# Two small products of a two-layer convolution kernel, with the weight matrix and the data exchanged on the tensor engine

## The chip, the cores and the metric

The kernel runs on one core of a Trainium2 chip. A core has a tensor engine (PE, which loads weights into its array, PEld, and streams a moving operand past them), a vector engine (DVE), a scalar engine (ACT), GpSimd (POOL) and a queue engine (SP) that here only issues DMAs. Matmul results land in PSUM, 8 banks of 128 partitions by 512 float32; everything else works in SBUF, 128 partitions wide. The metric is the device time of one execution in microseconds, the median of several runs. Everything is float32.

## What is computed

Two layers, on x of shape (4, 256, 256, 64): 4 images, height and width 256, 64 channels.

```python
# layer 0
h  = _pw(_ln(x, g1, b1), w_te, b_te)              # 64 -> 128 channels
F  = jnp.fft.fft2(h.astype(jnp.complex64), axes=(1, 2))
fr = jnp.concatenate([jnp.real(F), jnp.imag(F)], axis=-1)
fc = jax.nn.gelu(_pw(fr, w_fc, b_fc), approximate=False)
re, im = (fc[..., :HID], fc[..., HID:])
sp = jnp.real(jnp.fft.ifft2(re + 1j * im, axes=(1, 2)))
x1 = x + _pw(sp, w_tp, b_tp)                      # 128 -> 64 channels
h2 = _pw(_ln(x1, g2, b2), w_fe, b_fe)             # 64 -> 128 channels
d  = lax.conv_general_dilated(h2, w_dw, ...) + b_dw   # depthwise 3x3
d  = jax.nn.gelu(d, approximate=False)
x  = x1 + _pw(d, w_fp, b_fp)                      # 128 -> 64 channels
# layer 1: along the height, per channel
trend = _moving_average(x, 25); seasonal = x - trend
out   = trend + irfft(first 128 modes of rfft(seasonal), mixed by w_real + 1j * w_imag)
```

`_pw` is a product over the channels, `_ln` a layer norm. The change touches the two products that go from 128 to 64 channels: with `w_tp` and with `w_fp`.

## The kernel before

Transforms are products with tables. Products are exchanged where that is linear: the projection `w_tp` is applied before the inverse transform, and `b_fp` is added only at the end of layer 1. Four generators issue the work of layer 0 in pieces (each `yield` ends one):

- `forward_h` (L313 on): loads x, normalises, transforms along the height, writes `y_d` to HBM.
- `spectral` (L387 on): the transform along the width, the mix with `w_fc`, GELU, the projection, and the inverse transform along the width, into `u_d` in HBM. It works on groups of 4 rows, two *pairs* of rows a group (the first group has three, the first of them *special*: it holds rows whose spectrum is packed as two real ones). An image has 65 pairs.
- `convolution` (L588 on): the inverse transform along the height, the residual, layer norm, the depthwise convolution, GELU, the last product, and the residual, in 32 steps of 8 columns, into `x2_d` in HBM.
- `matrices`: the 64 matrices of layer 1, at the start.

Afterwards layer 1 runs as one loop over the channels (L912 on): it loads a matrix `mt` and the columns `xc` of `x2_d`, multiplies (L932), adds `b_fp` while it empties PSUM (L944 on ACT, L946 on DVE), and stores.

**Order.** PE, DVE, ACT and POOL execute exactly in the order in which the program issues (`manual_schedule`). `spaced` gives each piece of a generator an even position on a common axis, on which an image is 1.0 long, and `merge` always takes the generator that stands furthest back. The forward part of image b is spread from b - 2.05 to b - 1.1, its spectral part from b - 1.0 to b - 0.08 in 4 x 68 pieces, its convolution from b to b + 1 in 10 x 36 pieces. So the convolution of one image, the spectral part of the next and the forward part of the one after are merged.

**The spectral step.** Step i issues four pieces: `transform_w` of pair i with `fold` of pair i - 2; `back_w` of the group that pair i - 3 closes; `mix` of pair i - 1; and then, in one piece, `project` of pair i - 2, `activate` of pair i - 1 and, at a group's end, `negate` of the next group. `transform_w` (L435) multiplies a block [real, imaginary, -real] with the tables; `negate` (L422, ACT) writes the third part. `mix` (L455) makes four banks, which ACT (L467) and DVE (L472) bring to SBUF as `g`; `activate` (L478) is the GELU on ACT, `fold` (L485) an addition on DVE and a subtraction on POOL. `project` takes its two results, `dr` and `di`, 128 hidden channels by 512 positions each, as the *stationary* operand, 128 positions at a time, and streams `w_tp` (128 x 64) past them: the positions come out on the partitions, as `back_w` (L531) needs them. That is eight matmuls of 64 moving columns into one bank, which ACT copies into `zt` (L517). The special pair also adds the bias, by a matmul of `b_tp` with `at_dc`, a row with a single one.

**The convolution step.** Step q issues ten pieces: `back_h` of chunk q with the next load; `measure` (sums on DVE, the squares on ACT, L296); `conv_first` of chunk q - 3 (products L683 and L696 into four banks, emptied by ACT L715 and DVE L717, L718); `to_channels` of q - 1 (eight transposes L648 into two banks, copied by ACT L655); `norm`; `conv_rest` (L724); `finish` for the first half of chunk q - 4; `row_sums`; `conv_rest` and `edges`; and `activate` (GELU, L741) together with `finish` for the second half. `finish` also takes the data `gs` as the stationary operand, 128 positions at a time, and streams `w_fp` (128 x 64) past it: eight matmuls (L750) into one bank, in which the positions stand on the partitions. DVE adds `x1` on the way out of PSUM (L762), into a store tile that SP writes to `x2_d` (L771).

All tiles of PSUM come from one ring of eight banks (`bank`): a new tile takes the oldest bank, and the engine that fills it waits until that bank has been emptied.

Of the kernel before, what the change touches and what calls it, by code (L numbers as in the profile page):

```python
# [11 lines left out]
F32 = mybir.dt.float32  # L12
AF = mybir.ActivationFunctionType
ALU = mybir.AluOpType
# [4 lines left out]
P = 128  # L19
N = 256  # L20
C = 64
# [86 lines left out]
def conv_seq_kernel(ctx: ExitStack, tc: tile.TileContext, a: dict, tables: bass.AP, out: bass.AP):  # L108
    nc = tc.nc
# [9 lines left out]
    def bank(name):  # L119
        return psum.tile([P, 512], F32, tag="bank", name=name)  # L120
# [4 lines left out]
    def row(ap):  # L125
        return ap.rearrange("(o n) -> o n", o=1)

    def const(shape, name):
        return consts.tile(shape, F32, tag=name, name=name)
# [26 lines left out]
    w_tp = const([P, C], "w_tp")  # L156
    nw_tp = const([P, C], "nw_tp")
    b_tp = const([1, C], "b_tp")
    at_dc = const([1, P], "at_dc")
    w_fp = const([P, C], "w_fp")  # L160
    b_fp = const([P, C], "b_fp")

    wc_main = const([P, 2, 4, HID], "wc_main")
    wc_half = const([P, 4, HID], "wc_half")
# [5 lines left out]
    with tc.tile_pool(name="prep", bufs=1) as prep:  # L170
# [13 lines left out]
        nc.sync.dma_start(w_tp, a["w_tp"])  # L184
        nc.sync.dma_start(b_tp, row(a["b_tp"]))
        nc.sync.dma_start(w_fp, a["w_fp"])
        nc.sync.dma_start(b_fp, row(a["b_fp"]).to_broadcast([P, C]))

# [22 lines left out]
        nc.vector.tensor_scalar(v_dc, ps[:, 0:1], b_te, NPOS, ALU.add, ALU.mult)  # L213
        nc.vector.tensor_scalar(nw_tp, w_tp, -1.0, None, ALU.mult)
        nc.vector.tensor_scalar(b_tp, b_tp, 2.0 * NPOS, None, ALU.mult)
        nc.vector.memset(at_dc, 0.0)
        nc.vector.memset(at_dc[:, 0:1], 1.0)


        w_fe = prep.tile([P, HID], F32, tag="w_fe", name="w_fe")  # L220
# [166 lines left out]
    def spectral(b, pool):  # L387
# [1 line left out]
        y_d = y_ds.pop(b)  # L389
        u_d = spill.tile([P, N, 2, C], F32, tag="u_d", name=f"u_d_{b}")  # L390
        u_ds[b] = u_d
        KG = 4
        groups, per_group = {}, {}

        def load_group(g):
# [90 lines left out]
            pr["d"] = [gt[:, 0] for gt in pr["gts"]]  # L486

        def project(pr):
            dr, di = pr["d"]
            zt = groups[pr["g"]]  # L490
            ps = bank(f"ps_z_{pr['n']}")
            zv = ps.rearrange("p (j q c) -> p j q c", j=2, c=C)
            lhs = lambda d, j, t: d[:, j * N + t * P : j * N + (t + 1) * P]
            if pr["special"]:

                for t in range(2):
                    for r, terms in enumerate(
                        (((dr, 0, w_tp), (di, 1, nw_tp)), ((di, 0, w_tp), (dr, 1, w_tp)))
                    ):
                        dst = zv[:, 0, 2 * t + r, :]  # L500
                        bias = t == 0 and r == 0
                        for i, (d, j, w) in enumerate(terms):
                            nc.tensor.matmul(
                                dst, lhs(d, j, t), w, start=i == 0, stop=i == 1 and not bias
                            )
                        if bias:
                            nc.tensor.matmul(dst, at_dc, b_tp, start=False, stop=True)
                nb = 1
            else:
                nb = len(pr["blocks"])  # L510
                for r, d in enumerate((dr, di)):
                    for j in range(nb):
                        for t in range(2):
                            nc.tensor.matmul(  # L514
                                zv[:, j, 2 * t + r, :], lhs(d, j, t), w_tp, start=True, stop=True
                            )
            nc.scalar.copy(  # L517
                zt.rearrange("p t r k c -> p k (t r) c")[:, pr["slot"] : pr["slot"] + nb],
                zv[:, 0:nb],
            )  # L520

        def back_w(g):
# [38 lines left out]
                slot += 1 if prs[-1]["special"] else 2  # L561
        load_group(0)
        negate(0)
        for i in range(len(prs) + 3):
            if i < len(prs):
                pr = prs[i]
                pr["blocks"] = per_group[pr["g"]][pr["i"]]
                transform_w(pr)
                if pr["last"] and pr["g"] + 1 < NG:
                    load_group(pr["g"] + 1)  # L570
            if 0 <= i - 2 < len(prs):
                fold(prs[i - 2])
            yield
            if 0 <= i - 3 < len(prs) and prs[i - 3]["last"]:
                back_w(prs[i - 3]["g"])
            yield
            if 0 <= i - 1 < len(prs):
                mix(prs[i - 1])
            yield
            if 0 <= i - 2 < len(prs):  # L580
                project(prs[i - 2])
            if 0 <= i - 1 < len(prs):
                activate(prs[i - 1])
            if i < len(prs) and prs[i]["last"] and prs[i]["g"] + 1 < NG:
                negate(prs[i]["g"] + 1)
            yield

    def convolution(b, pool):  # L588
# [1 line left out]
        u_d = u_ds.pop(b)  # L590
        W = 8
        NCH = N // W
        TD, XN = 4, 1
        NP = W // 2
        x1s, ucs, var, xns, ts, stores = {}, {}, {}, {}, {}, {}
        rows = lambda t: t.rearrange("p t w c -> p (t w) c")

        def load(q):
# [31 lines left out]
        def measure(q):  # L630
            var[q] = statistics(pool, rows(x1s[q]), f"c_{b}_{q}")
# [94 lines left out]
        def edges(q):  # L726
            for par, g in enumerate(gs[q]):
                lo, hi = 0, NP
                if q == 0 and par == 0:
                    nc.vector.tensor_tensor(g[:, 0], g[:, 0], edge_cols[:, 0], ALU.add)  # L730
                    lo = 1
                if q == NCH - 1 and par == 1:
                    hi = NP - 1
                    nc.vector.tensor_tensor(g[:, hi], g[:, hi], edge_cols[:, 1], ALU.add)
                ends = g[:, lo:hi, 0 : N : N - 1]
                nc.vector.tensor_tensor(ends, ends, edge_rows[:, lo:hi], ALU.add)  # L736

        def activate(q):
            for g in gs[q]:
# [3 lines left out]
        def finish(q, i0):  # L743

            ps = bank(f"ps_f_{b}_{q}_{i0}")
            pv = ps.rearrange("p (t w c) -> p t w c", t=2, c=C)
            for t in range(2):
                for i in range(2):
                    for par in range(2):
                        nc.tensor.matmul(  # L750
                            pv[:, t, 2 * i + par, :],
                            gs[q][par][:, i0 + i, t * P : (t + 1) * P],
                            w_fp,
                            start=True,
                            stop=True,
                        )
            s, w0 = divmod(q * W + 2 * i0, SW)
            if s not in stores:
                stores[s] = pool.tile([P, 2, C, SW], F32, tag="st", name=f"st_{b}_{s}")
            x1 = x1s[q]  # L760
            for t in range(2):
                nc.vector.tensor_tensor(  # L762
                    stores[s][:, t, :, w0 : w0 + 4].rearrange("p c w -> p w c"),
                    x1[:, t, 2 * i0 : 2 * i0 + 4, :],
                    pv[:, t],
                    ALU.add,
                )
            if w0 + 4 == SW:
                st = stores.pop(s)
                for t in range(2):  # L770
                    nc.sync.dma_start(  # L771
                        x2_d[b, t * P : (t + 1) * P, s], st[:, t]
                    )

        load(0)
        for q in range(NCH + 4):
            new, before = q < NCH, 0 <= q - 1 < NCH
            now, old = 0 <= q - 3 < NCH, 0 <= q - 4 < NCH
            if new:
                back_h(q)  # L780
            if q + 1 < NCH:
                load(q + 1)
            yield
            if new:
                measure(q)
            yield
            if now:
                conv_first(q - 3)
            yield
            if before:  # L790
                to_channels(q - 1)
            yield
            if new:
                norm(q)
            yield
            if now:
                conv_rest(q - 3, 0)
            yield
            if old:
                finish(q - 4, 0)  # L800
            yield
            if before:
                row_sums(q - 1)
            yield
            if now:
                conv_rest(q - 3, 1)
                edges(q - 3)
            yield
            if now:
                activate(q - 3)  # L810
            if old:
                finish(q - 4, 2)
                del gs[q - 4], x1s[q - 4]
            yield

# [76 lines left out]
    with (  # L892
        in_order,
        tc.tile_pool(name="fwd", bufs=2) as fwd,
        tc.tile_pool(name="mix", bufs=2) as mixing,
    ):
        at = {
            all_batches(spectral, mixing, 4 * 68, -1.0, -0.08): -1.0,
            all_batches(forward_h, fwd, 4 * 33, -2.05, -1.1): -2.05,
        }  # L900
        with tc.tile_pool(name="matrices", bufs=2) as pool:
            at[spaced(matrices(pool), C + 2, -2.05, -1.1)] = -2.05
            merge(at, -1.0)
        with tc.tile_pool(name="conv", bufs=2) as conv:
            at[all_batches(convolution, conv, 10 * 36, 0.0, 1.0)] = 0.0
            merge(at, float(B + 1))


    with tc.tile_pool(name="seq", bufs=2) as pool:
        CG = 8  # L910
        CM, CO = 4, 2
        nb2 = max(1, B // 2)  # L912
        nf = nb2 * N
        mt = xc = oc = None
        for c in range(C):
            if c % CM == 0:
# [75 lines left out]
```

## Time and profile before

| | us |
|---|---|
| median of 5 runs | 5806.86 (5805.03 to 5808.17) |
| the profiled execution | 5807.93 |
| its span, first to last instruction | 5806.1 |
| TensorE busy / share | 5400.8 / 93% |
| mean granted TensorE clock | 0.956 |

The span falls into stages, which can be told from what runs: up to 400 us the setup, the matrices of layer 1 and the first forward part; from 400 to 1200 the spectral part of image 0 with the forward part of image 1, without a convolution; from 1200 to 4640 convolution, spectral part and forward part merged; from 4640 to 5320 the last convolution alone; then layer 1.

How the profile is read: a group's row gives line, engine, operation, output and inputs by the program's names, the shape (weights as rows*columns, then the moving operand), the count, then busy time and the mean duration of one, and then the idle time of the engine just before the group and what ended it. Consecutive matmuls overlap, so the mean of one is longer than its share of the busy time. A row of the order of time gives start, length, engine, line, and in brackets the idle time before. The granted clock is the share of full speed at which TensorE's clock ran.

### The profile page before, as it was taken

The page shows a single profiled execution, that of the slowest core. Times are in us where ns is not written, and L with a number is a line of the kernel's source. Part 1 is how long each engine was busy: PE and PEld are TensorE (multiplying, and loading weights), DVE is VectorE, ACT ScalarE, POOL GpSimd, SP SyncE. Part 2 cuts the span into 40 slices and gives each one's busy share as a digit, 9 for nine tenths or more (in the row PEclk, how much of TensorE's full clock was granted, in tenths as well). Part 3 has the DMA queues.
Part 4 walks back from the last instruction along what each step waited for, and adds up shares of the span by engine and source line. Part 5 has one row for each costly group of instructions (what it writes and reads, how often), then busy time and mean ns, then how long its engine had stood idle before and what let it go on. Part 6 is the DMA issues. An engine that isn't in the chain of part 4 may idle for free. (4 is left out here: it accounts for less than half of the span.)

```text
span 5806.1 us, 72361 instructions
## 1 busy us (share of the span) xinstructions
PE 5400.8 (93%) x27467; PEld 3475.8 (60%) x27467; DVE 3945.6 (68%) x6043; ACT 2341.3 (40%) x3294; POOL 1636.8 (28%) x778
## 2 busy tenths in 40 slices
PE   8988788889999999899999999999999999997999
PEld 4456565556666666566666666666666656664444
DVE  6766565688777877777778875676666678884221
ACT  2335454444444444444444443444444422221111
POOL 3443333343333332333333331222222222220000
PEclk9988888899999999899999999999999999998999
DMA  5543232323233323323233322122222222224998
GB/s 164 174 158 95 77 98 84 104 86 103 94 99 103 108 84 102 97 88 101 89 106 102 102 79 89 62 80 73 77 77 73 70 84 88 88 83 137 333 327 268
DMA packets 654914, 653.71 MB, mean 113 GB/s; under 512 B 31117, under 2 KB 506719, under 8 KB 654440
## 3 DMA queue, kind: packets, MB, share of 16 engines
q1 hardware_dynamic: 654568, 649.09, 35.2%
q8 instruction: 218, 3.57, 0.3%
q14 instruction: 128, 1.05, 0.1%
HBM read 363.76 MB, written 285.21 MB: 112 GB/s over the span
## 5 line engine op out<-in xcount | busy, mean ns | idle before, releaser
L485 POOL TENSOR_TENSOR g<-g 128x512 f32<-128x512 f32 x260 | 364.0, 1400 | 2376.0 <-ACT g L478 2291.6
L683 PE MATMUL ps_h<-td,wc_main 128*128 128x512 f32 x2048 | 1010.6, 616 | 4.5 <-DVE st L762 2.0
L435 PE MATMUL ps_x<-tab,yb 128*128 128x128 f32 x4064 | 629.8, 312 | 240.4 <-ACT yb L422 240.3
L472 DVE TENSOR_TENSOR g<-ps_p,g 128x512 f32<-128x512 f32 x1040 | 688.6, 683 | 120.2 <-ACT g L467 102.3
L435 PEld LDWEIGHTS ps_x<-tab,yb 128*128 128x128 f32 x4064 | 566.2, 220 | 292.6 <-ACT yb L422 262.9
L696 PEld LDWEIGHTS ps_h<-td,wc_half 64*128 64x128 f32 x4032 | 408.1, 186 | 460.5 <-issue 388.8
L478 ACT ACTIVATE g<-g,b_fc 128x1024 f32<-128x1024 f32 (+1 forms) x520 | 573.4, 1139 | 57.5 <-DVE g L472 56.6
L306 POOL TENSOR_TENSOR rstd_c<-var_c,minus_half 128x16 f32<-128x16 f32 x128 | 379.2, 2963 | 768.8 <-DVE var_c L300 758.4
L696 PE MATMUL ps_h<-td,wc_half 64*128 64x128 f32 (+1 forms) x4032 | 582.3, 405 | 2.0 <-DVE td L668 2.0
L683 PEld LDWEIGHTS ps_h<-td,wc_main 128*128 128x128 f32 x2048 | 359.6, 195 | 355.6 <-issue 241.3
L514 PEld LDWEIGHTS ps_z<-w_tp,g 128*128 128x128 f32 x4064 | 480.9, 194 | 142.7 <-issue 34.6
L514 PE MATMUL ps_z<-w_tp,g 128*128 128x64 f32 x4064 | 512.6, 280 | 27.0 <-DVE g L485 25.2
L750 PEld LDWEIGHTS ps_f<-w_fp,h 128*128 128x128 f32 x4096 | 486.1, 194 | 56.0 <-ACT g L467 18.2
L750 PE MATMUL ps_f<-w_fp,h 128*128 128x64 f32 x4096 | 513.5, 279 | 5.3 <-ACT h L741 5.3
L455 PE MATMUL ps_p<-xs,wp 64*128 64x512 f32 (+1 forms) x2080 | 511.4, 607 | 2.0 <-DVE h L724 1.8
L531 PE MATMUL ps_u<-zt,tab 128*128 128x256 f32 x2048 | 494.3, 397 | 1.4 <-ACT zt L517 1.4
L741 ACT ACTIVATE h<-h,b_conv 128x1024 f32<-128x1024 f32 x256 | 279.9, 1141 | 531.3 <-DVE h L736 531.3
L932 PE MATMUL ps_o<-xc,mt 128*128 128x512 f32 x1024 | 448.5, 600 | 42.3 <-issue 21.8
L306 POOL TENSOR_TENSOR rstd<-var,minus_half 128x16 f32<-128x16 f32 x128 | 399.4, 3120 | 302.5 <-DVE var L300 226.3
L467 ACT COPY g<-ps_p 128x512 f32<-128x512 f32 (+1 forms) x520 | 294.9, 582 | 468.1 <-PE ps_p L455 461.9
L724 DVE TENSOR_TENSOR h<-h,ps_h 128x512 f32<-128x512 f32 x512 | 328.2, 682 | 222.1 <-PE ps_h L696 222.1
L531 PEld LDWEIGHTS ps_u<-zt,tab 128*128 128x128 f32 x2048 | 399.1, 200 | 78.2 <-issue 12.6
(120 smaller groups left out, 6694.4 us busy)
## 6 DMA issues: line engine op xcount, KB each, us to landing
xt<-in_x_dram SPq DMA_DIRECT2D x256, 256.0 KB, 3.3
y_d<-yt SPq DMA_DIRECT2D x256, 256.0 KB, 3.4
x_c<-in_x_dram SPq DMA_DIRECT2D x128, 512.0 KB, 4.7
yb<-y_d SPq DMA_DIRECT2D x256, 256.0 KB, 3.2
u_d<-ut SPq DMA_DIRECT2D x256, 256.0 KB, 2.5
uc_c<-u_d SPq DMA_DIRECT2D x128, 512.0 KB, 4.6
x_d<-st SPq DMA_DIRECT2D x128, 512.0 KB, 4.2
xc<-x_d SPq DMA_DIRECT2D x64, 1024.0 KB, 10.3
```

The source lines that it names most:

```text
L306: nc.gpsimd.tensor_tensor(rstd, var, minus_half.to_broadcast([P, n]), ALU.pow)
L435: nc.tensor.matmul(ps[:, j * N + t * P : j * N + (t + 1) * P], blk[:, t, k, lo : lo + 2 * C], tb[:, t, :], start=i == 0, stop=i == 1,)
L455: nc.tensor.matmul(ps[:, :nf], wp[rows, cols], rhs[rows], start=True, stop=r == 1 or not pr["special"],)
L472: nc.vector.tensor_tensor(gt[:, i, :nf], re, gt[:, 1, :nf], op)
L478: nc.scalar.activation(g, g, AF.Gelu, bias=b_fc[:, half : half + 1])
L485: eng.tensor_tensor(g[:, 0], g[:, 0], g[:, 1], op)
L514: nc.tensor.matmul(zv[:, j, 2 * t + r, :], lhs(d, j, t), w_tp, start=True, stop=True)
L531: nc.tensor.matmul(ps[:, r * KG * C : (r + 1) * KG * C], tb[:, t, :], zt[:, t, ri].rearrange("p k c -> p (k c)"), start=ri == 0, stop=ri == 1,
L683: nc.tensor.matmul(pss[par], wc_main[:, par, k, :], ts[q][:, k].rearrange("p j i -> p (j i)"), start=True, stop=False,)
L696: nc.tensor.matmul(pss[par][:, s * P : (s + n) * P], wc_half[lo : lo + C, k, :], td[lo : lo + C, k, at : at + n, :].rearrange("p j i -> p ...
L750: nc.tensor.matmul(pv[:, t, 2 * i + par, :], gs[q][par][:, i0 + i, t * P : (t + 1) * P], w_fp, start=True, stop=True,)
L932: nc.tensor.matmul(ps[:, :nf], mt[:, c % CM, t, to * P : (to + 1) * P], xc[:, t, b0 : b0 + nb2, :, c % CG, :], start=t == 0, stop=t == 1,)
```

## The change

In both products the operands change places. The weight matrix, 64 columns wide, becomes the stationary operand, and 512 positions stream past it. The two results that `project` makes (from `dr` and `di`), and the two that `finish` makes (even and odd columns), go to partitions 0 to 63 and 64 to 127 of one bank. The channels then stand on the partitions and not the positions, so ACT copies the bank to SBUF (`zs`, `fs`, one buffer each), and four transposes with the identity turn it into a second bank. From that one, ACT copies to `zt` as before (`turn`), or DVE adds `x1` as before (`store`).

`turn` is a piece of its own, one step after its `project`, between `mix` and `project`, so that a spectral step has five pieces, the pipeline is one step longer, and `back_w` comes a step later. In the convolution `finish` of the first half moves to the piece of `measure` and its `store` to that of `to_channels`; `finish` of the second half moves to the place where the first half's was, and its `store` to the place of the second half's `finish`. The number of pieces of a convolution step stays ten. `b_fp` gives up its place among the constants and is loaded when layer 1 begins; `at_dc` shrinks to one element.

```diff
-    at_dc = const([1, P], "at_dc")
+    at_dc = const([1, 1], "at_dc")
...
-    b_fp = const([P, C], "b_fp")
...
-        nc.sync.dma_start(b_fp, row(a["b_fp"]).to_broadcast([P, C]))
...
         def project(pr):
+
             dr, di = pr["d"]
-            zt = groups[pr["g"]]
             ps = bank(f"ps_z_{pr['n']}")
...
             else:
-                nb = len(pr["blocks"])
+                nf = pr["nf"]
                 for r, d in enumerate((dr, di)):
-                    for j in range(nb):
-                        for t in range(2):
-                            nc.tensor.matmul(
-                                zv[:, j, 2 * t + r, :], lhs(d, j, t), w_tp, start=True, stop=True
-                            )
+                    nc.tensor.matmul(
+                        ps[r * C : (r + 1) * C, :nf], w_tp, d[:, :nf], start=True, stop=True
+                    )
+            zs = pool.tile([P, 512], F32, tag="zs", name=f"zs_{pr['n']}", bufs=ZS)
+            nc.scalar.copy(zs[:, :nf], ps[:, :nf])
+            pr["zs"] = zs[:, :nf]
+
+        def turn(pr):
+
+            zt, zs = groups[pr["g"]], pr["zs"]
+            nf = zs.shape[1]
+            ps = bank(f"ps_zt_{pr['n']}")
+            for i in range(nf // P):
+                nc.tensor.transpose(ps[:, i * P : (i + 1) * P], zs[:, i * P : (i + 1) * P], ident)
+            nb = nf // N
             nc.scalar.copy(
                 zt.rearrange("p t r k c -> p k (t r) c")[:, pr["slot"] : pr["slot"] + nb],
-                zv[:, 0:nb],
+                ps[:, :nf].rearrange("p (j q c) -> p j q c", j=nb, c=C),
             )
...
-        for i in range(len(prs) + 3):
+        for i in range(len(prs) + 4):
...
-            if 0 <= i - 3 < len(prs) and prs[i - 3]["last"]:
-                back_w(prs[i - 3]["g"])
+            if 0 <= i - 4 < len(prs) and prs[i - 4]["last"]:
+                back_w(prs[i - 4]["g"])
             yield
             if 0 <= i - 1 < len(prs):
                 mix(prs[i - 1])
+            yield
+            if 0 <= i - 3 < len(prs):
+                turn(prs[i - 3])
             yield
             if 0 <= i - 2 < len(prs):
                 project(prs[i - 2])
...
         def finish(q, i0):
 
             ps = bank(f"ps_f_{b}_{q}_{i0}")
+            for par in range(2):
+                nc.tensor.matmul(
+                    ps[par * C : (par + 1) * C],
+                    w_fp,
+                    gs[q][par][:, i0 : i0 + 2, :].rearrange("p j h -> p (j h)"),
+                    start=True,
+                    stop=True,
+                )
+            fs = pool.tile([P, 2, 2, P], F32, tag="fs", name=f"fs_{b}_{q}_{i0}", bufs=FS)
+            nc.scalar.copy(fs.rearrange("p i t h -> p (i t h)"), ps)
+            ends[q, i0] = fs
+
+        def store(q, i0):
+
+            fs = ends.pop((q, i0))
+            ps = bank(f"ps_ft_{b}_{q}_{i0}")
             pv = ps.rearrange("p (t w c) -> p t w c", t=2, c=C)
             for t in range(2):
                 for i in range(2):
-                    for par in range(2):
-                        nc.tensor.matmul(
-                            pv[:, t, 2 * i + par, :],
-                            gs[q][par][:, i0 + i, t * P : (t + 1) * P],
-                            w_fp,
-                            start=True,
-                            stop=True,
-                        )
+                    nc.tensor.transpose(
+                        pv[:, t, 2 * i : 2 * i + 2, :].rearrange("p w c -> p (w c)"),
+                        fs[:, i, t],
+                        ident,
+                    )
...
             if new:
                 measure(q)
+            if old:
+                finish(q - 4, 0)
             yield
             if now:
                 conv_first(q - 3)
             yield
             if before:
                 to_channels(q - 1)
+            if old:
+                store(q - 4, 0)
             yield
...
             if old:
-                finish(q - 4, 0)
+                finish(q - 4, 2)
             yield
...
             if now:
                 activate(q - 3)
             if old:
-                finish(q - 4, 2)
+                store(q - 4, 2)
                 del gs[q - 4], x1s[q - 4]
             yield
...
-            all_batches(spectral, mixing, 4 * 68, -1.0, -0.08): -1.0,
+            all_batches(spectral, mixing, 5 * 69, -1.0, -0.08): -1.0,
...
+        b_fp = pool.tile([P, C], F32, tag="b_fp", name="b_fp", bufs=1)
+        nc.sync.dma_start(b_fp, row(a["b_fp"]).to_broadcast([P, C]))
```

In the special pair the four products are rewritten in the same way (256 moving columns, the two halves of the partitions), and the bias becomes a matmul of `b_tp` with the single element.

## The prediction

> **What bounds the kernel now.** I read the page's busy line first, then busy time by stage, then the groups of instructions, the waits of TensorE in the long stage, and last the order of time around the edited blocks.
>
> ```profile
> PE 5400.8 (93%) x27467; PEld 3475.8 (60%) x27467; DVE 3945.6 (68%) x6043; ACT 2341.3 (40%) x3294; POOL 1636.8 (28%) x778
> ```
>
> TensorE is the only engine near its span. The same by stage (busy of PE, weight load, DVE, ACT, POOL; then the granted clock):
>
> ```profile
> 400.00:1200.00 800.00, 657.21 (x3504) 477.77 (x3505) 488.89 (x698) 403.70 (x582) 278.62 (x141) 0.86 0.29 91
> 1200.00:4640.00 3440.00, 3291.16 (x18434) 2223.84 (x18434) 2556.58 (x3957) 1542.55 (x2161) 1031.56 (x496) 0.97 0.28 89
> 4640.00:5320.00 680.00, 656.96 (x3387) 398.94 (x3386) 515.55 (x863) 188.66 (x247) 155.11 (x65) 0.98 0.24 81
> 5320.00:5806.00 486.00, 448.53 (x1024) 195.97 (x1024) 96.00 (x128) 87.94 (x128) 0.00 (x0) 0.96 1.00 309
> ```
>
> From 400 to 1200 the spectral part of image 0 runs without a convolution to fill its waits: 143 us of idle TensorE and a clock of 0.86. From 1200 to 4640 spectral part and convolution are merged, with 149 us idle. After that the last convolution runs alone, and then the second layer, which the change touches only by one small load. So a microsecond of TensorE work saved between 1200 and 5300 is a microsecond of time, unless a wait takes it.
>
> **The two edited blocks.** Busy time and mean of one, by group: the two blocks that go, and the two nearest rows to what comes.
>
> ```profile
> L750 PE MATMUL ps_f<-w_fp,h 128*128 128x64 f32 x4096 | 513.5, 279 | 5.3 <-ACT h L741 5.3
> L514 PE MATMUL ps_z<-w_tp,g 128*128 128x64 f32 x4064 | 512.6, 280 | 27.0 <-DVE g L485 25.2 <-POOL g L485 1.7
> L355 PE MATMUL ps_y<-xt,tab 128*64 128x512 f32 x1024 | 293.5, 628 | 25.4 <-DVE xt L345 19.3 <-issue 3.1 <-DMA x_c<-in_x_dram 1.9
> L648 PE MATMUL ps_t<-ident,xn_c 128*128 128x128 f32 x1024 | 139.5, 280 | 9.8 <-POOL xn_c L307 9.7
> ```
>
> A matmul of float32 is two instructions here (8 matmuls per call of finish, 256 calls, 4096 instructions); a transpose is one. L355 is the very form that the change introduces: 64 weight columns, 512 moving columns, the two results on the two halves of one bank's partitions. In order of time, TensorE's blocks and then the weight loads of L355:
>
> ```profile
> 2045.30 2.00 PE L750 MATMUL ps_f<-w_fp,h 128*128 128x64 f32 x16
> 2047.13 1.95 PE L514 MATMUL ps_z<-w_tp,g 128*128 128x64 f32 x16
> 2048.92 1.94 PE L683 MATMUL ps_h<-td,wc_main 128*128 128x512 f32 x4
> ...
> 2055.85 1.94 PE L355 MATMUL ps_y<-xt,tab 128*64 128x512 f32 x8
> 2057.72 0.48 PE L531 MATMUL ps_u<-zt,tab 128*128 128x256 f32 x1
> ```
>
> ```profile
> 2056.34 0.14 PEld L355 LDWEIGHTS ps_y<-xt,tab 128*64 128x64 f32 x2 [0.29 <-DVE h L724]
> 2056.76 0.14 PEld L355 LDWEIGHTS ps_y<-xt,tab 128*64 128x64 f32 x2 [0.28 <-issue]
> ```
>
> From start to next start, finish takes 2047.13 - 2045.30 = 1.83 us and project 2048.92 - 2047.13 = 1.79: 1.81. The eight instructions of L355 take 2057.72 - 2055.85 = 1.87 and step in pairs 0.42 to 0.43 apart, one of each half, side by side. Four of them: 1.87 - 2 x 0.43 = 1.01. Eight transposes of L648 run from 2072.76 to the next block at 2073.69, 0.93; four are 0.47 to 0.50, taken as 0.48. So a call goes from 1.81 to 1.49 and saves 0.32. By busy time: 16 x 126 ns (513.5/4096) = 2.01 against 4 x 287 (293.5/1024) + 4 x 136 = 1.69, also 0.32; this holds the stretches at the lower clock. I take 0.33 (0.30 to 0.345). Calls: 254 full projects and 256 finishes, 510 x 0.33 = **-168 us** (-153 to -176). The four special projects hardly count.
>
> [...]
>
> **ScalarE's new copies.** One more 128x512 copy out of PSUM per call, 514 x 0.58 us (L517's copies in the order of time) = 298 us, 2341 to 2639, 45% of the span. Hidden behind TensorE, since the transposes are put at least two pieces of the program later than the copy; without that cover they would cost 0.58 each, 298 us. They matter where ScalarE's order does, next.
>
> **The wait for the negated columns.** In the long stage TensorE's waits are nearly all one:
>
> ```profile
> PE ps_x L435 <- ACT yb L422: 133.6, 62, 6.0
> ...
> PE ps_h L683 <- DVE x_c L628: 1.3, 4, 0.4
> ```
>
> At a group's end project, activate and negate are issued in one piece, and ScalarE works them off in order; the next piece of the spectral part is transform_w, which needs negate:
>
> ```profile
> 2083.89 0.58 ACT L517 COPY zt<-ps_z 128x512 f32<-128x512 f32 x1 [3.03 <-PE ps_z L514]
> 2084.37 2.19 ACT L478 ACTIVATE g<-g,b_fc 128x1024 f32<-128x1024 f32 x2
> 2086.47 0.62 ACT L422 ACTIVATE yb<-yb 128x512 f32<-128x512 f32 x1
> ```
>
> ```profile
> 2083.69 0.44 PE L435 MATMUL ps_x<-tab,yb 128*128 128x128 f32 x2
> 2087.14 3.35 PE L435 MATMUL ps_x<-tab,yb 128*128 128x128 f32 x14 [3.00 <-ACT yb L422]
> ```
>
> From the project's end this chain is the copy, two GELUs and negate, and TensorE waits 3.0 us less whatever the convolution has between. The chain keeps its length (the copy to zs replaces the copy to zt), but the cover shrinks. The spectral part is spread over 0.92 of an image's time in 4 x 68 pieces, now in 5 x 69: a piece every 0.92/272 = 0.00338, then 0.92/345 = 0.00267, against the convolution's 1/360 = 0.00278. Between two spectral pieces lie 1.22 pieces of the convolution, then 0.96. TensorE time of its ten pieces, from the same rows: 1.82 (back_h), 0, 5.9, 0.93, 0, 2.95, 1.83, 0, 2.95, 1.83; afterwards 1.82, 1.01, 5.9, 1.41, 0, 2.95, 1.01, 0, 2.95, 0.48. The wait 3.0 less cover, averaged over one piece, is 1.48 before and 1.54 after; over two neighbours 0.46 before. Before: 0.78 x 1.48 + 0.22 x 0.46 = 1.26; after 0.96 x 1.54 + 0.04 x 3.0 = 1.60. Three images with 31 boundaries each: 117 to 149. Going through the pieces in merge's own order instead gives 121 to 162; measured are 134, so the account holds. I take **+40** (+25 to +60).
>
> **PSUM banks.** The eight banks go round. A finish's bank was emptied by DVE, now by ScalarE behind the Square of measure (L296, 1.06 us), which waits for DVE's L628; behind it in ScalarE's queue are the copies of conv_first, which DVE waits for. Today L683 already waits for the two banks of back_h, six times (L624 and L628), 2.4 us in all; the finish's bank comes next in the ring and is free Square and copy, 1.06 + 0.58 = 1.64, later. And the ring turns faster: 16 banks per convolution step for 14, 8 per pair for 7. Bounds: -2 (the waits for DVE's L762 go) to 128 steps x 1.64 = 210. Since only 6 of 96 steps touch it now, I take ten steps of 1.6: **+16**.
>
> **The clock.** At 0.97 the long stage loses 3% of 3440, 103 us, and the lower stretches come with the waits. Waits 40/134 longer would add 31; the new matmuls fill the array better than 64-column ones, which may take it back. **+10** (-20 to +31).
> [...]
>
> **Ends.** Image 0's spectral part gets one copy, four transposes and a copy longer before the convolution can start (0.58 + 0.48 + 0.58), the last finishes have no work between copy and transposes (some 0.8 twice), and b_fp's load stands ahead of the first mt on SP's queue (0.4, like L918's 0.37 issue): **+4**. The removed memset and the load at the start are hidden behind the other loads.
>
> **Sum.** -168 + 40 + 16 + 10 + 4 = -98. The profiled execution took 5807.9 with a span of 5806.1; the median is 5806.9, which I start from: **5709**. Its own range goes from -176 + 25 - 20 + 3 to -153 + 60 + 70 + 31 + 6: 5639 to 5821, most of it below 5790.
>
> **Rivals.** (1) The waits do not grow: 5807 - 168 + 4 = 5643. For it: where DVE binds the chain, the extra piece between mix and activate gives it more time. Against: in most boundaries the chain begins at the project's end, as shown. (2) Slower: ScalarE's late release of finish's bank. At the full 1.64 in all 128 steps, 5709 + 194 = 5903; it decides from (98 + 16)/128 = 0.89 us per step. For it: ScalarE stands in line behind DVE, which is 74% busy in the long stage, and the ring is shorter. Against: only 2.4 us of such waits now, and from 4640 on, with no spectral part, there is none at all. (3) The change doesn't do what it says: the halves run one after the other, two more steps of 0.43 per call, 510 x 0.86 = 439, 6148. Against: L355 does it, 287 ns busy for each instruction where L683's full-width ones take 493 (1010.6/2048).
>
> **Numbers.** A measurement of this kernel tells about 0.2% (12 us) from no change. Chances: forecast 0.62 (0.58 faster, 0.03 same, 0.01 slower), rival 1 0.13, rival 2 0.20 (of it 0.01 faster and 0.02 same, where the bank's price stays near the deciding point), rival 3 with any other loss 0.05. Faster 0.72, same 0.05, slower 0.23. The range 5635 to 5850 leaves out about a twentieth below and the upper part of rival 2 and rival 3 above.
>
> **What would show it.** Project and finish as 4 matmul instructions of 128x512 at about 290 ns busy, plus 4 transposes at 136; TensorE's busy time some 165 lower; the wait on L422 near 175 in the long stage; waits of the convolution's first products on ScalarE small (rival 2: over 100 us); clock of the long stage within 0.95 to 0.98. The forecast is wrong if the matmuls show 490 ns each, if transposes wait for fs or zs, or if idle TensorE grows by over 110 us.

## The result, and the profile after

The changed kernel takes 5819.02 us (median of 23 runs) against 5806.1 (43 runs of the kernel before beside it): the ratio is 1.0022, 95% interval 1.0016 to 1.0027. It is a little slower, by 0.2%. The profiled execution has a span of 5811.3 us against 5806.1, a difference of 5.2 us where the medians differ by 12.9.

The page's busy line after, and from the groups of TensorE the four that replace L514 and L750:

```profile
PE 5305.6 (91%) x23371; PEld 2874.3 (49%) x23371; DVE 3934.5 (68%) x6042; ACT 2606.7 (45%) x3810; POOL 1625.4 (28%) x778
```

```profile
L755 PE MATMUL ps_f<-h,w_fp 128*64 128x512 f32 x1024 | 336.2, 638 | 40.4 <-ACT h L749 34.7 <-ACT ut L546 1.9 <-DVE st L783 0.2
L507 PE MATMUL ps_z<-g,w_tp 128*64 128x512 f32 x1008 | 269.2, 612 | 3.0 <-DVE g L482 1.8 <-DVE h L732 1.1
L520 PE MATMUL ps_zt<-ident,zs 128*128 128x128 f32 x1024 | 167.3, 285 | 0.9 <-DVE ut L548 0.9
L773 PE MATMUL ps_ft<-ident,fs 128*128 128x128 f32 x1024 | 160.8, 280 | 6.0 <-ACT fs L763 5.7 <-DVE g L469 0.3
```

TensorE does less: 95 us less busy (5400.8 to 5305.6), and 600 us less of weight loads. `project` costs 269.2/1008 = 267 ns for each of its instructions, where the full-width ones of L691 take 1020.6/2048 = 498, so the halves of the array do work side by side; `finish` costs 336.2/1024 = 328, which is a first sign. Yet the span did not fall, so TensorE stands idle 100 us more. Its longest waits over the whole span say where:

```profile
PE ps_x L432 <- ACT yb L419: 316.0, 102, 8.5
PE ps_f L755 <- ACT h L749: 34.7, 17, 4.0
```

The wait for `negate` (now L419) was 240.3 us and is 316.0; the wait of `finish` for the convolution's GELU (L749) was 5.3 and is 34.7. The wait at the start of layer 1 hardly changed: 42.3 us before (L932), 43.5 after (L959).

By stage, from the first `back_h` of one image to that of the next:

| us (idle TensorE) | before | after |
|---|---|---|
| start to the first convolution | 1148 | 1097 |
| image 0 merged | 1208 (58) | 1221 (89) |
| image 1 merged | 1219 (57) | 1219 (90) |
| image 2 merged | 1129 (47) | 1137 (79) |
| image 3, the last convolution | 607 (13) | 642 (29) |

So 51 us are won before the first convolution, and 56 are lost again behind it. The last convolution shows why most plainly, since nothing else runs there. TensorE, after, in order of time:

```profile
4905.93 1.99 PE L624 MATMUL ps_s_c<-uc_c,tab 64*128 64x512 f32 x8
4908.05 2.11 PE L755 MATMUL ps_f<-h,w_fp 128*64 128x512 f32 x4
4910.09 1.98 PE L691 MATMUL ps_h<-td,wc_main 128*128 128x512 f32 x4
...
4920.30 1.08 PE L755 MATMUL ps_f<-h,w_fp 128*64 128x512 f32 x4
4921.31 1.98 PE L691 MATMUL ps_h<-td,wc_main 128*128 128x512 f32 x4
...
4924.87 1.13 PE L624 MATMUL ps_s_c<-uc_c,tab 64*128 64x512 f32 x4
```

and ScalarE in the same stretch:

```profile
4906.85 2.19 ACT L749 ACTIVATE h<-h,b_conv 128x1024 f32<-128x1024 f32 x2 [3.73 <-DVE h L744]
```

The second half's `finish` takes 4921.31 - 4920.30 = 1.01 us, to the hundredth what was forecast. The first half's, at 4908.05, takes 2.04 (to 4910.09) and starts 2.12 after `back_h` started, which needs 1.82: the change moved it up to the piece after `back_h`, directly behind the GELU of the same chunk. One GELU (even columns) ends at about 4908.0, the other (odd columns) at 4909.0; the two halves of the product each wait for one, and so no longer run side by side. A step takes 4924.87 - 4905.93 = 18.94 us. The kernel before takes 4925.67 - 4907.29 = 18.38, from its `back_h` to the next:

```profile
4907.29 1.99 PE L616 MATMUL ps_s_c<-uc_c,tab 64*128 64x512 f32 x8
...
4925.67 1.99 PE L616 MATMUL ps_s_c<-uc_c,tab 64*128 64x512 f32 x8
```

### The profile page after: what moved, and what is told of

Its sections match the earlier page's. It is cut to its first block, busy times and chain, and to the rows that moved or that the text cites. A ratio compares the mean times of both kernels' runs of the same rounds, so it can differ in the third digit from the quotient of the medians.

```text
span 5811.3 us, 64784 instructions
## 1 busy us (share of the span) xinstructions
PE 5305.6 (91%) x23371; PEld 2874.3 (49%) x23371; DVE 3934.5 (68%) x6042; ACT 2606.7 (45%) x3810; POOL 1625.4 (28%) x778
## 4 chain that ended last, share of the span: by engine, by line
PE 75%; DVE 12%; ACT 6%; issue 4%; DMA 2%; SPq 0%; POOL 0%; ACTq 0%; DVEq 0%; POOLq 0%
PE ps_h L691 15%; PE ps_x L432 9%; PE ps_h L704 8%; PE ps_o L959 7%; PE ps_p L452 7%; PE ps_u L536 7%; PE ps_f L755 5%; PE ps_y L352 4%; PE ps_z L507 3%; ACT g L475 3%; PE ps_s_c L624 3%; DVE g L469 2%; DVE xt L342 2%; PE ps_zt L520 2%; PE ps_ft L773 2%
## 5 line engine op out<-in xcount | busy, mean ns | idle before, releaser
L691 PE MATMUL ps_h<-td,wc_main 128*128 128x512 f32 x2048 | 1020.6, 622 | 1.6 <-DVE x_c L636 1.6
L432 PE MATMUL ps_x<-tab,yb 128*128 128x128 f32 x4064 | 645.6, 317 | 316.5 <-ACT yb L419 316.0
L691 PEld LDWEIGHTS ps_h<-td,wc_main 128*128 128x128 f32 x2048 | 361.6, 196 | 437.9 <-issue 312.8
L452 PE MATMUL ps_p<-xs,wp 64*128 64x512 f32 (+1 forms) x2080 | 534.0, 626 | 2.7 <-DVE h L732 2.0
L732 DVE TENSOR_TENSOR h<-h,ps_h 128x512 f32<-128x512 f32 x512 | 328.3, 683 | 296.1 <-PE ps_h L704 295.8
L959 PE MATMUL ps_o<-xc,mt 128*128 128x512 f32 x1024 | 447.8, 600 | 43.5 <-DMA xc<-x_d 42.5
L536 PE MATMUL ps_u<-zt,tab 128*128 128x256 f32 x2048 | 470.3, 383 | 1.5 <-ACT zt L522 1.5
L725 DVE TENSOR_TENSOR h<-h,ps_h 128x512 f32<-128x512 f32 x256 | 175.4, 685 | 388.9 <-PE ps_h L704 353.8
L536 PEld LDWEIGHTS ps_u<-zt,tab 128*128 128x128 f32 x2048 | 378.9, 190 | 80.8 <-issue 12.1
L749 ACT ACTIVATE h<-h,b_conv 128x1024 f32<-128x1024 f32 x256 | 280.0, 1141 | 293.3 <-DVE h L744 293.3
L755 PE MATMUL ps_f<-h,w_fp 128*64 128x512 f32 x1024 | 336.2, 638 | 40.4 <-ACT h L749 34.7
L973 DVE TENSOR_SCALAR oc<-ps_o,b_fp 128x512 f32<-128x512 f32 x128 | 96.1, 751 | 393.2 <-PE ps_o L959 302.3
L959 PEld LDWEIGHTS ps_o<-xc,mt 128*128 128x128 f32 x1024 | 195.7, 192 | 295.2 <-issue 285.9
```

The lines of the kernel that those rows point to most:

```text
L432: nc.tensor.matmul(ps[:, j * N + t * P : j * N + (t + 1) * P], blk[:, t, k, lo : lo + 2 * C], tb[:, t, :], start=i == 0, stop=i == 1,)
L452: nc.tensor.matmul(ps[:, :nf], wp[rows, cols], rhs[rows], start=True, stop=r == 1 or not pr["special"],)
L536: nc.tensor.matmul(ps[:, r * KG * C : (r + 1) * KG * C], tb[:, t, :], zt[:, t, ri].rearrange("p k c -> p (k c)"), start=ri == 0, stop=ri == 1,
L691: nc.tensor.matmul(pss[par], wc_main[:, par, k, :], ts[q][:, k].rearrange("p j i -> p (j i)"), start=True, stop=False,)
L732: nc.vector.tensor_tensor(g, g, m, (ALU.add, ALU.subtract)[r])
L755: nc.tensor.matmul(ps[par * C : (par + 1) * C], w_fp, gs[q][par][:, i0 : i0 + 2, :].rearrange("p j h -> p (j h)"), start=True, stop=True,)
```

## The experiments

The times of stages and the waits, in us, are TensorE's in the profiled run of each kernel. The ratios are against runs of the kernel before made beside each set, whose medians were 5807 (up to "before, negate first"), 5802 (up to "turn with project") and 5802; times from different sets differ by those 5 us, too.

| kernel | median, us | ratio to before, interval | to first convolution | images 0 to 2 | last convolution | wait for negate | wait of finish for GELU |
|---|---|---|---|---|---|---|---|
| before | 5806 | | 1148 | 3556 | 607 | 240 | 5 |
| after | 5819 | 1.0022 (1.0016 to 1.0027) | 1097 | 3577 | 642 | 316 | 35 |
| finish later | 5770 | 0.9938 (0.9923 to 0.9953) | 1096 | 3578 | 592 | 329 | 8 |
| negate first | 5486 | 0.9451 (0.9436 to 0.9465) | 972 | 3372 | 638 | 98 | 36 |
| both | 5443 | 0.9374 (0.9358 to 0.9389) | 971 | 3376 | 595 | 106 | 8 |
| before, negate first | 5544 | 0.9549 (0.9535 to 0.9564) | 1038 | 3399 | 609 | 55 | 5 |
| project's half alone | 5795 | 0.9990 (0.9981 to 0.9999) | 1094 | 3592 | 609 | 301 | 5 |
| finish's half alone | 5870 | 1.0116 (1.0101 to 1.0131) | 1145 | 3586 | 638 | 258 | 48 |
| before, finish early | 6122 | 1.0555 (1.0538 to 1.0573) | 1143 | 3738 | 737 | 258 | 147 |
| turn with project | 5735 | 0.9887 (0.9872 to 0.9902) | 1095 | 3502 | 638 | 266 | 35 |
| all moves | 5337 | 0.9198 (0.9182 to 0.9214) | 957 | 3284 | 594 | 12 | 8 |
| before, negate sooner | 5465 | 0.9418 (0.9404 to 0.9432) | 996 | 3364 | 607 | 15 | 5 |
| all moves, fs by VectorE | 5355 | 0.9227 (0.9213 to 0.9240) | 961 | 3304 | 595 | 12 | 8 |

The theory after the result, called M in the expectations: the blocks save what they should, and the order in which the pieces are issued eats it, at two waits. Rival R: the exchange itself gains nothing.

**Finish later.** The first half's `finish` behind `conv_first`, its `store` behind the first `conv_rest`.

```diff
             if new:
                 measure(q)
-            if old:
-                finish(q - 4, 0)
             yield
             if now:
                 conv_first(q - 3)
+            if old:
+                finish(q - 4, 0)
...
```

> The changed kernel with one thing moved: the first half's finish goes from the piece of measure to the end of the piece of conv_first, and its store to the piece of the first conv_rest; all else as changed. Theory M (the block saving is real, and order eats it): the GELU of the same chunk (2.2 us) is then covered by back_h and conv_first; a step of the convolution alone falls from 18.95 us to about 17.8, which is 38 us over the last image, and some 20 more where it is merged: 5765 (5745 to 5785). [...]

Measured 5770, 49 us faster than the changed kernel and 36 faster than the kernel before, so rival R falls. In the last convolution, TensorE:

```profile
4900.18 1.88 PE L691 MATMUL ps_h<-td,wc_main 128*128 128x512 f32 x4
...
4903.65 1.08 PE L755 MATMUL ps_f<-h,w_fp 128*64 128x512 f32 x4
4904.66 1.98 PE L691 MATMUL ps_h<-td,wc_main 128*128 128x512 f32 x4
...
4916.10 1.08 PE L755 MATMUL ps_f<-h,w_fp 128*64 128x512 f32 x4
4917.11 1.09 PE L656 MATMUL ps_t<-ident,xn_c 128*128 128x128 f32 x8
4918.04 1.88 PE L691 MATMUL ps_h<-td,wc_main 128*128 128x512 f32 x4
```

Both calls of `finish` now take 1.01, and a step 4918.04 - 4900.18 = 17.86 us: the forecast of 17.8 held. In the merged images nothing was won, where 20 us had been expected: there the wait of `finish` fell by 16 us, but the wait for `negate` grew by 13, and TensorE's idle time stayed (258 and 259 us).

**Negate first.** In the changed kernel.

```diff
-            if 0 <= i - 1 < len(prs):
-                activate(prs[i - 1])
             if i < len(prs) and prs[i]["last"] and prs[i]["g"] + 1 < NG:
                 negate(prs[i]["g"] + 1)
+            if 0 <= i - 1 < len(prs):
+                activate(prs[i - 1])
```

> The changed kernel with negate issued before activate in the last piece of the spectral step; all else as changed. Theory M: the chain that TensorE waits for at a group's end loses the two GELUs, 3.3 us become 1.2, and the wait of transform_w for negate falls from 316 us to under 100; the lower stretches of the clock go with it: 5640 (5560 to 5700). Rival W (the wait only moves to the fold and the project behind it, since the GELUs come 0.6 us later): the wait for negate goes, but waits of project for fold grow by as much, 5790 to 5820.

Measured 5486, below the range of M: the mechanism was right, the size too small. The wait for `negate` fell to 98:

```profile
PE ps_x L432 <- ACT yb L419: 98.3, 71, 6.4
```

No other came in its place (`project` waits 13 us for `fold`), so rival W falls. With the waits went the stretches at half clock, from 507 us of the run to 183.

**Both moves**, and **the kernel before with negate first**, the control.

> The changed kernel with both moves of the two runs before. Theory M: the two gains add, 5585 (5510 to 5650), and it is faster than the kernel before with the same move of negate by about 60 to 130 us, since the block saving of 0.3 us per call is then not eaten. Rival R: not faster than the kernel before with that move, within 15 us of it or slower.

> The kernel before, with negate issued before activate and nothing else changed. Theory M: its wait for negate falls from 240 us to under 70, and the clock's lower stretches become fewer: 5630 (5570 to 5700). Rival W: the wait moves to project, 5780 to 5806.

Measured 5443 and 5544. Both are faster than their ranges, and the exchange is worth 101 us between them. Rival R falls: with less in its way the exchange does gain.

**Each half alone.** `project` and `turn` with the old convolution; the new `finish` and `store` with the old spectral part.

> Only the spectral half of the change (project, turn, five pieces per step); the convolution is that of the kernel before. Theory M: the first spectral stage gains the 50 us that the changed kernel shows there, the merged stages lose some 9 per image to the longer wait for negate and the lower clock behind it, the last convolution is unchanged at 607: 5780 (5755 to 5800). Rival R (the products themselves gain nothing): 5806 or above.

> Only the convolution's half of the change (finish and store in their new pieces); the spectral part is that of the kernel before. Theory M: nothing in the first spectral stage, the last convolution goes from 607 to about 642 as in the changed kernel, the merged stages gain little: 5830 (5810 to 5850). Rival R: the loss is the same in merged and lone stages, since it lies in the products and copies.

Measured 5795 and 5870. The first lies in its range, but it is only 7 us below the runs of the kernel before beside it, just clear of no change. `project`'s half gains 54 us before the first convolution and gives 36 of them back in the merged images, more than the 27 expected. `finish`'s half costs 31 us in the last convolution and 30 in the merged ones, so it is not nearly neutral there, and the forecast was 40 too low. Rival R, the same loss with and without a merged spectral part, doesn't hold either: 31 us in the lone image, 10 in each merged one. The two together (-7 and +68 against the runs of before beside them) would make +61; the changed kernel has +13. The halves don't add; the pieces meet in other places when both are there, but what that does was not followed up.

**The kernel before with its own finish early.** No exchange, only the place.

```diff
             if new:
                 measure(q)
+            if old:
+                finish(q - 4, 0)
             yield
...
             if old:
-                finish(q - 4, 0)
+                finish(q - 4, 2)
             yield
```

> The kernel before, with its own finish (no exchange, no transposes) of the first half moved to the piece of measure and that of the second half to where the first's was, as the change places them. Theory M (the place behind the GELU costs, not the exchange): TensorE stands some 2 us per step until both GELUs are done, 32 x 2.2 = 70 us in the last convolution, little where it is merged: 5875 (5840 to 5910). Rival: the place does not matter, 5806 within 10.

Measured 6122, 320 us slower where 70 were expected. ScalarE and TensorE in its last convolution, of one step:

```profile
5103.02 2.19 ACT L741 ACTIVATE h<-h,b_conv 128x1024 f32<-128x1024 f32 x2 [8.68 <-DVE h L736]
...
5104.22 0.43 PE L750 MATMUL ps_f<-w_fp,h 128*128 128x64 f32 x2 [1.34 <-ACT h L741]
...
5105.26 1.77 PE L750 MATMUL ps_f<-w_fp,h 128*128 128x64 f32 x14 [0.60 <-ACT h L741]
...
5124.48 0.43 PE L750 MATMUL ps_f<-w_fp,h 128*128 128x64 f32 x2 [1.34 <-ACT h L741]
```

The step is 5124.48 - 5104.22 = 20.26 us where the clock is full, so 1.9 longer, as thought: 60 us. But that image takes 130 us longer: TensorE runs 150 us of it at half clock, where the kernel before has 17, which can account for up to 67 us more. The granted clock of the whole run falls from 0.956 to 0.931. With these waits the clock falls, too, and the merged images lose 182 us. The place alone, without any exchange, costs far more than the whole change shows. With the exchange in the same places (`finish`'s half alone) the loss is 68 and not 320; the `finish` behind the wait is shorter there, and transposes stand in the piece that `finish` left empty, but which of the two helps was not separated.

**Turn with project.** One piece in place of two, so four pieces per spectral step (`4 * 69`).

> The changed kernel with turn and project in one piece, so that a spectral step has four pieces as before (4 x 69). Theory M: between the end of a group and the next transform_w lie 1.2 pieces of the convolution again instead of 0.96, the wait for negate in the merged stage falls from 200 us towards 145, with some of the clock: 5755 (5725 to 5790). Rival W (the longer wait comes from ScalarE's longer queue, not from the spacing): 5810 to 5825.

Measured 5735. The wait for `negate` in the merged images fell from 211 to 161 and the images by 75 us together. So the extra piece cost 50 us of this wait, and rival W falls for most of it. Whether it does so by the cover that the forecast counted is looked at below.

**All moves, and the same order without the exchange.** `finish` later, four pieces, and `negate` at the head of the last piece; the kernel before with `negate` in that place.

```diff
+            if i < len(prs) and prs[i]["last"] and prs[i]["g"] + 1 < NG:
+                negate(prs[i]["g"] + 1)
             if 0 <= i - 3 < len(prs):
                 turn(prs[i - 3])
-            yield
             if 0 <= i - 2 < len(prs):
                 project(prs[i - 2])
             if 0 <= i - 1 < len(prs):
                 activate(prs[i - 1])
-            if i < len(prs) and prs[i]["last"] and prs[i]["g"] + 1 < NG:
-                negate(prs[i]["g"] + 1)
             yield
```

> The exchange kept, with the order mended in all places found: finish of the first half behind conv_first, four pieces per spectral step, and negate at the head of the last piece, before turn, project and activate. Theory M: the wait for negate, still 119 us with the earlier moves, falls to about 40, and half of the rest of the lower clock goes: 5370 (5330 to 5410). Rival (what is left is bound by ScalarE's queue): 5430 or above.

> The kernel before with negate at the head of the last piece, before project and activate: the same mended order without the exchange. Theory M: 5520 (5490 to 5545); with the waits out of both, the exchange is worth its blocks, 510 x 0.30 = 150 us (120 to 170), between this run and the one with all moves. Rival R: under 100 us between them.

Measured 5337 and 5465. The first beats both kernels, at 0.9198 of the time before. Its busy line and the two waits:

```profile
PE 5121.2 (96%) x23371; PEld 2750.7 (52%) x23371; DVE 3943.6 (74%) x6042; ACT 2591.1 (49%) x3810; POOL 1639.0 (31%) x778
```

```profile
PE ps_z L507 <- DVE g L482: 26.2, 14, 4.0
...
PE ps_x L432 <- ACT yb L419: 11.8, 14, 2.2
```

With both waits out of the way the exchange is worth 5465 - 5337 = 128 us, in the forecast range, below the 150 that 510 blocks of 0.30 make.

**fs copied by VectorE**, in that best version.

> As with all moves, but fs is copied by VectorE and not by ScalarE: it tells whether the copies in ScalarE's queue hold up the rest. Theory M: within 15 us of the run with all moves, VectorE 5% busier. Rival Q (ScalarE's queue costs): 25 to 60 us faster.

Measured 5355, 18 us slower, a little outside the 15. So rival Q falls: ScalarE's copies of `fs` don't hold up the rest, and VectorE, already 74% busy, is the worse place for them.

## Why the prediction was wrong

- **The blocks: right in mechanism, too large.** The product takes 1.01 us as forecast. Four transposes, by the median from start to next start at full clock, take 0.53 in `store` and 0.58 in `turn`, not 0.48; the old blocks take 1.83. So a call saves 0.24 to 0.30 and not 0.33: about 138 us and not 168. Between the two kernels with mended order, 128 arrive.
- **The step that failed: the move of `finish` was costed at nothing.** The prediction checked what comes behind the moved `finish` ("the transposes are put at least two pieces of the program later than the copy") but not what the `finish` itself waits for. Between the GELU of a chunk and its first `finish` there had been `back_h`, `conv_first`, `to_channels` and `conv_rest`, over 10 us of TensorE work; the change leaves `back_h`, 1.8, against GELUs of 2.2 that in the last convolution start 0.9 after it. The sum has no term for that. Moving it back wins 49 us (finish later), 43 with `negate` mended. It shows in the busy time, too, which fell by 95 us and not by 165: by the groups' rows `project`'s block lost 76 (512.6 against 269.2 + 167.3), `finish`'s only 17 (513.5 against 336.2 + 160.8).
- **The wait for `negate`: the second step that failed, about half the size.** Forecast +40 in the merged images; measured there 143 to 211, +67, and over the whole span 316.0 - 240.3 = +76. The count was of cover behind a chain that begins at the project's end. What it lacked is ScalarE's order in front of that chain: in the longest waits the copy to `zs` itself starts late. Of the 71 waits in the merged images, 15 have a copy that starts over 0.5 us after the project's end, 9 of them behind the convolution's GELU, which waits for VectorE. These 15 make 78 us; before, 8 such waits made 28. All the others make 132, before 115. So 50 of the 67 us are late copies, and 17 are left for the cover that the forecast counted as 32 to 41. Putting the piece back takes 35 us off the late copies and 15 off the others: the piece did matter, but mostly in another way than counted. After, ScalarE and then TensorE:

```profile
1506.85 2.19 ACT L749 ACTIVATE h<-h,b_conv 128x1024 f32<-128x1024 f32 x2 [4.44 <-DVE h L744]
...
1508.95 0.56 ACT L511 COPY zs<-ps_z 128x512 f32<-128x512 f32 x1
...
1509.41 2.19 ACT L475 ACTIVATE g<-g,b_fc 128x1024 f32<-128x1024 f32 x2
...
1511.50 0.61 ACT L419 ACTIVATE yb<-yb 128x512 f32<-128x512 f32 x1
...
1512.17 1.22 PE L432 MATMUL ps_x<-tab,yb 128*128 128x128 f32 x4 [8.51 <-ACT yb L419]
```

  `project` had ended at 1503.2 in this case, and ScalarE stood idle for 4.44 us in front of the other stream's GELU. That is a wait of 8.5 us where the account allowed 3.0 at most. The warning stood in the line that the prediction shows: its 62 waits before have a longest of 6.0.
- **The clock: +10 forecast, about 0 in sum, but of two large parts.** From 391 us to the first convolution TensorE ran 218 us at half clock, in the changed kernel 144; the forecast had no term for that stage. In the merged images together it was 206 before and 263 after, so up to 28 us are lost there, within the forecast range of -20 to +31.
- **The banks: +16 forecast, next to nothing measured.** TensorE waits 1.6 us for the banks of `back_h`, 2.4 before, and the transposes wait 5.7 us for `fs`. Rival 2 forecast a slower kernel by a wait on ScalarE, and both came, but not at the ring of banks that it named.
- **The ends: +4 forecast.** The wait at the start of layer 1 is nearly the same, 42.3 and 43.5.
- **Rival 3** (the halves don't run side by side) is excluded by 267 ns an instruction, except where two GELUs kept them apart.
- **The sum.** Taken one by one, these differences (30 for the blocks, 49 for the place of `finish`, 36 for `negate`, less 30 for banks, clock and ends) make some 85 of the 111 us between -98 and +13. They overlap, since a wait that goes in one place can come back in another, so the rest has no single place in the runs.

How the gain was lost follows from pairs of runs. Between the best orders the exchange wins 128 us (5465 against 5337). With `negate` behind `project` and five pieces, it wins 101 (5544 against 5443): 27 gone to the spacing and ScalarE's order. With `finish` early as well, 58 (5544 against 5486): 43 gone to the place behind the GELU. With `negate` behind the GELUs, as both original kernels have it, it loses 13: another 71, since the kernel before loses 262 us by that order and the changed one 333. Both waiting and clock have a part in it: with `negate` first, the wait for it falls by 218 us in the changed kernel and by 185 in the kernel before, and the time at half clock by 324 and 249 us.

## What to carry to other kernels

When engines execute in a fixed order, an edit that shortens a block and moves it has two prices. For each block that changes its place, list what it waits for and how much work of its engine lies between that and the new place, not only what comes behind it. And where an engine waits for another engine's queue, look first at what stands in that queue in front of the result: here a copy with a sign, issued before two GELUs and not behind them, was worth 260 to 330 us, at least twice what the faster product is worth at best.

## What the runs showed of the hardware

The granted clock in the record is either full or half: 78 stretches of the profiled run before are at half clock, and 95 of the one after. It moved with the waits: from 0.956 over the whole run before to 0.931 with `finish` early, where a step of the last convolution is 1.9 us longer, and to 0.988 in the best version. The prediction guessed that the kind of matmul matters, too. The stretch from 400 to 950 us is spectral work without a convolution in both kernels with `negate` first; before with that move, and then the exchange with both moves (busy times of PE, weight load, DVE, ACT, POOL, then the clock):

```profile
400.00:950.00 550.00, 502.50 (x2837) 362.82 (x2835) 377.54 (x539) 321.31 (x463) 210.35 (x107) 0.92 0.33 101
```

```profile
400.00:950.00 550.00, 514.49 (x2729) 306.12 (x2729) 439.34 (x613) 396.79 (x594) 241.44 (x121) 1.00 0.37 113
```

TensorE is idle 47.5 and 35.5 us of 550, but the clock is 0.92 with the products of 64 moving columns and 1.00 with those of 512: 89 us and 3 us of the stretch ran at half clock. A part of this can be the length of the waits, of which the longest are 3.59 us in the first and 1.97 in the second. The same stretch in the kernel before and in the changed one, with `negate` behind the GELUs in both:

```profile
400.00:950.00 550.00, 460.68 (x2474) 339.03 (x2474) 328.80 (x473) 281.57 (x407) 182.85 (x94) 0.86 0.29 89
```

```profile
400.00:950.00 550.00, 459.26 (x2204) 280.47 (x2202) 352.31 (x497) 325.37 (x482) 196.44 (x100) 0.89 0.31 93
```

TensorE is idle 89.3 and 90.7 us, with longest waits of 4.6 and 6.4 us, and the clock is 0.86 and 0.89: 155 us and 119 us at half clock. So with the exchange the clock was higher at nearly the same idle time. The time up to the first convolution gets 67 us shorter by the exchange with `negate` first (1038 to 971), over three times the 65 blocks of 0.30. No run here changes the kind of matmul alone, so how much of this is its doing was not shown. Over the whole run the mean clock was 0.956 before and after: it rose from 0.86 to 0.90 between 391 us and the first convolution and fell from 0.97 to 0.96 in the merged images and from 0.99 to 0.98 in the last.
